# A transformer block with adapters on one core: the prologue's transfers, tables and first products in another order

## Chip, cores, metric

One core of a Trainium2 chip runs the whole program. The metric is the device time in microseconds; three executions of the kernel before took 955.52, 958.76 and 960.24 us, the median is 958.76. Engines: TensorE (PE) multiplies, VectorE (DVE), ScalarE (ACT) and GpSimd (POOL) work elementwise, SyncE (SP) issues DMA transfers.

## The reference

Eight sequences of 512 tokens with 256 features pass four layers. The first is a transformer layer whose normalisation is modulated by an embedding of a time step; then come an adapter chosen by a domain index, a rotation of groups of four features by two angles, and a second adapter. Cut to what matters here, with `_ln` a normalisation without weights:

```python
# layer 0; x is (8, 512, 256), 16 heads of 16
e = steps / 100 * 4000 * freqs                   # (8, 128)
emb = concat([sin(e), cos(e)])                   # (8, 256)
ada = silu(emb) @ W_ada + b_ada                  # (8, 512): scale, shift
h = _ln(x) * (1 + scale) + shift
q, k, v = h @ Wq + bq, h @ Wk + bk, h @ Wv + bv
s = q @ k.T / 4 + bias                           # bias is (8, 16, 512, 512)
s = where(mask, -inf, s)
x = h + softmax(s) @ v @ Wo + bo
# feed-forward with x * sigmoid(1.702 x); then the layers:
x = adapter1(x, domain); x = rotate(x, theta, phi); x = adapter3(x, domain)
```

## The kernel before

Work on attention is cut into 128 units: a sequence b, a group g of four heads and a tile qt of 128 queries. A unit loads four bias tiles of 128x512 (L856, 256 KB each), POOL adds the masked keys' large negative value (`neg`, L860), PE computes four scores matrices (L868), DVE subtracts them from the bias and takes row minima (L879), ACT takes the exponential (L883), the result is turned (by PE at L918, or by DVE at L894 and a transfer), and PE multiplies by the values (L944). After eight units half a sequence is complete, and `finish` runs the output projection, the feed-forward part and both adapters over it. While one sequence's units run, `prepare(b + 1)` makes q, k and v of the next.

Two parts set the order. The first lines (L286 to L328) are issued as they stand: SP's transfers of the first sequence, the small inputs and the first weights, memsets on POOL, `halves` on DVE. From `plan = Plan()` on, everything is a task of a planner: `plan(engine, cost, emit, reads, writes, mode, at)` notes a task with a cost in us, a `rank` (lower goes first), and where given an earliest time `at`. `plan.run` replays the engines as clocks that begin at the times in its argument and gives each free engine the ready task of lowest rank; DMA stands for SP's queue. `mode` adds a cost where an engine changes kind of work. `begin` and `end(first, last)` spread the ranks of the tasks between them. The result is one list, and each engine executes its instructions in that order: an instruction that waits holds all behind it on its engine. Weights are loaded into space that later holds other things: `first` is a view of a `pT` tile, with W_ada, Wq and Wk side by side.

The prologue's tasks by name. `embedding`: the token numbers are cast (`tokf`, L380), spread over partitions by a product with ones (L381), multiplied by frequencies and reduced to within pi (`reduced`, L387 to L395), then `sines` takes Sin twice, Square and Identity (L401 to L404), and a Tanh makes silu of it (L409, `emb` at L411). Filling products of the identity (`rows_of_identity`, L373) keep PE busy. `modulation`: `emb` by W_ada (L435), its sum with `b_ada` (L442), four transposes (L449) into columns `modc`. `constants`: bias columns `bk` and `bqh` (L469 to L477), and `dense`, which POOL uses to close the padding between heads in Wq and Wk (L492). `prepare(0)`: statistics of each token tile (L653, L655), the reciprocal root on POOL (L660 to L662), normalising on ACT (L675), transposes by PE (L739), modulation into `xT`, and into a turned copy `xTp` used for v (L753 on ACT, L755 on DVE), then for each of two chunks c of 128 padded columns q and k: products (L766), `qz` in two halves (L772) and `kT` (L782); then v (L803, L814) and `neg` from the mask (L819). Units of groups 0 and 1 read chunk 0, groups 2 and 3 chunk 1. `experts_matrices` gathers the adapters' expert weights (L1161 to L1197).

The compiler puts a table load (ACT_TABLE_LOAD) ahead of an activation whose function isn't in the table at hand.

Of the kernel before, what the change touches and what calls it, by code (L numbers as in the profile page):

```python
# [19 lines left out]
P = 128  # L20
# [195 lines left out]
def conditioned_sequence_kernel(  # L216
# [33 lines left out]
    def slots(name, count, shape, dtype=F32):  # L250
# [38 lines left out]
    nc.vector.memset(ang[:, B:], 0.0)  # L289
    nc.sync.dma_start(RES.tiles[0][:, :2], x0[:, :2])  # L290
    nc.sync.dma_start(cols, cols_in)
    nc.sync.dma_start(tok_i[:, :B], steps[None, :])
# [4 lines left out]
    nc.sync.dma_start(ang[:B, B:], angles.rearrange("(j b) -> b j", j=2))  # L297
    nc.sync.dma_start(tok_i[:, B:], domain[None, :])
    nc.sync.dma_start(
        SIG.tiles[0][:B].rearrange("p r d -> p (r d)"), rows_in[: 2 * D].partition_broadcast(B)  # L300
    )
    nc.sync.dma_start(first[:, 1], w_q.rearrange("(c p) n -> p c n", p=P))
    nc.sync.dma_start(first[:, 2], w_k.rearrange("(c p) n -> p c n", p=P))
# [16 lines left out]
    nc.gpsimd.memset(ones, 1.0)  # L320
    neg_half = const.tile([P, NT], F32, tag="neg_half", name="neg_half")
# [40 lines left out]
    def embedding():  # L362
# [6 lines left out]
        plan.rank = -4.9  # L369
# [5 lines left out]
        for _ in range(20):  # L375
            plan(PE, 0.28, rows_of_identity, [], [warm], mode="full")
# [3 lines left out]
        plan(DVE, 0.2, lambda: nc.vector.tensor_copy(tokf, tok_i), [], ["tokf"], at=4.2)  # L380
# [16 lines left out]
        plan(DVE, 1.2, reduced, [], [scr], at=5.0)  # L397

        def sines():
# [10 lines left out]
            th.t, sc[:, :, :B], AF.Tanh, scale=0.5), ["sc"], [th], mode="exp")  # L410
# [13 lines left out]
    def modulation():  # L424
# [5 lines left out]
            b_ada.t[:, 0], b_ada.t[:, 0], AF.Identity, bias=1.0), [], [b_ada], at=7.0)  # L430
# [8 lines left out]
        plan(PE, 2.2, product, ["emb"], [ps], mode="full", at=7.5)  # L439
# [20 lines left out]
    def constants():  # L460
# [5 lines left out]
            [], [further], mode="full", at=4.0)  # L466
# [15 lines left out]
        plan(DVE, 0.6, biases, [further], ["bk", "bqh"], at=4.2)  # L482

        for c in range(NC):
            for n, w in ((1, wq), (2, wk)):
# [8 lines left out]
                plan.rank = -9.0 + 0.1 * (n + 2 * c)  # L494
                plan(POOL, 0.55, dense, [], [("w", n, c)], at=7.5 + 1.2 * n)


        for i, v_pad in enumerate(VP.tiles):

            def clear(v_pad=v_pad):  # L500
                nc.gpsimd.memset(v_pad, 0.0)
                nc.gpsimd.memset(heads_of(v_pad)[:, :, :, HD : HD + 1], 1.0)

            plan.rank = -10.0
            plan(POOL, 2.0, clear, [], [("ones", i)])
# [11 lines left out]
    def late_weights():  # L517
# [6 lines left out]
        load(-2.5, 0.75, lambda: nc.sync.dma_start(  # L524
            wv, w_v.rearrange("(c p) n -> p c n", p=P)), "wv")
        load(-2.4, 0.4, lambda: nc.sync.dma_start(
# [803 lines left out]
```

## Time and profile before

| What | Measured |
|---|---|
| median of three executions | 958.76 us |
| the profiled execution, its time | 961.32 us |
| its span on the core | 959.6 us |
| mean granted PE clock | 0.987 |
| PE from 20 to 25 us | 4.54 of 5 us busy |
| PE from 25 to 30 us | 5.00 of 5 us busy |
| PE from 800 us to the end | 139.99 of 160 us busy |
| table loads on ACT | 1 each for L514, L401, L409; 27 for L1058, 26 for L883; 1283 ns each |
| first scores (L868) start | 24.91 us |
| scores of the ninth unit start | 67.0 us |

A row of the timeline has the start in us, the duration, the engine, the line and operation, what is written and read, the shape, how many instructions were joined, and in brackets the idle time of the engine before it with what ended it. A matrix product in float32 counts as two records. "PE busy" comes from modelled ends of products and overlaps with weight loads (PEld). The chain is followed back from the last instruction to what released each step, so a step on it is one that nothing else hid.

### The profile page before, as it was taken

What the parts mean: (1) busy time and instruction counts of PE and PEld (TensorE: products, weight loads), DVE (VectorE), ACT (ScalarE), POOL (GpSimd) and SP (SyncE); (2) the same over time, 40 slices, a digit from 0 to 9 for tenths busy, and PEclk for the clock granted to TensorE, in tenths of its full rate; (3) what the DMA queues carried; (4) which work ended last, traced back from release to release, by engine and by line L of the source; (5) the groups of instructions that cost most, each with busy time, mean ns of one, the idle gap of its engine ahead of it and who ended that gap; (6) DMA issues with size and microseconds to landing.
All of it is one profiled execution on the core that took longest, in us unless ns stands there. A gap on an engine that the chain in (4) does not pass through costs nothing.

```text
span 959.6 us, 21049 instructions
## 1 busy us (share of the span) xinstructions
PE 905.8 (94%) x6646; PEld 596.1 (62%) x6646; DVE 799.7 (83%) x2162; ACT 748.8 (78%) x1359; POOL 754.9 (79%) x841
## 2 busy tenths in 40 slices
PE   7999999999899999999999999999999999899993
PEld 4655765676565665666656665666656666566782
DVE  3786789987988889988898879987899888888755
ACT  5896879786887869879698778977788786897542
POOL 7788999787877969778887878878687886988222
PEclk9999999999999999999999999999999999999997
DMA  8579586987768787787969878688776978878000
GB/s 289 174 250 285 182 281 179 282 265 237 213 184 273 248 257 208 231 273 228 276 175 271 259 233 259 182 277 258 212 229 198 280 211 271 249 220 267 26 17 23
DMA packets 158945, 214.25 MB, mean 223 GB/s; under 512 B 18479, under 2 KB 90201, under 8 KB 158834
## 3 DMA queue, kind: packets, MB, share of 16 engines
q1 hardware_dynamic: 158834, 212.91, 73.2%
q8 instruction: 53, 0.87, 0.4%
q14 instruction: 58, 0.48, 0.1%
HBM read 149.89 MB, written 4.24 MB: 161 GB/s over the span
## 4 chain that ended last, share of the span: by engine, by line
PE 51%; DVE 16%; ACT 10%; POOL 7%; DMA 7%; issue 5%; SPq 1%; DVEq 0%; POOLq 0%; ACTq 0%
PE bank L1024 9%; PE bank L868 8%; PE bank L918 8%; PE bank L944 7%; PE bank L999 6%; DMA bias<-in_bias 6%; POOL bias L860 4%; DVE bias L879 4%; ACT bias L883 3%; PE bank L766 3%; DVE tb L894 3%; PE bank L711 2%; PE bank L803 2%; PE bank L1052 2%; PE bank L687 2%
## 5 line engine op out<-in xcount | busy, mean ns | idle before, releaser
L860 POOL TENSOR_TENSOR bias<-bias,neg 128x512 f32<-128x512 f32 x512 | 581.7, 1163 | 118.5 <-DMA bias<-in_bias 83.3
L883 ACT ACTIVATE bias<-bias,low 128x512 f32<-128x512 f32 x512 | 343.1, 720 | 67.7 <-DVE low L879 67.0
L879 DVE CUSTOM_DVE_ANT_0 bias<-bank,bias 128x512 f32<-128x512 f32 x512 | 326.7, 684 | 56.5 <-PE bank L868 49.4
L918 PE MATMUL bank<-shifted,bias 128*128 128x128 f32 x1152 | 160.9, 278 | 15.3 <-DVE inv L970 8.7
L918 PEld LDWEIGHTS bank<-shifted,bias 128*128 128x128 f32 x1152 | 128.9, 141 | 69.0 <-issue 16.9
L894 DVE STREAM_TRANSPOSE tb<-bias 128x512 f32<-128x512 f32 x224 | 150.1, 694 | 7.5 <-ACT bias L883 6.9
L868 PE MATMUL bank<-kT,qz 32*128 32x512 f32 x1024 | 156.0, 640 | 0.0
L645 ACT COPY pT<-bank 128x512 f32<-128x512 f32 x209 | 114.9, 586 | 30.8 <-PE bank L918 27.3
L944 PE MATMUL bank<-pT,v_pad 128*32 128x256 f32 x2048 | 125.0, 385 | 4.3 <-issue 1.4
L999 PE MATMUL bank<-hT,w 128*128 128x256 f32 (+1 forms) x544 | 123.5, 371 | 0.8 <-ACT pT L645 0.8
L1024 PE MATMUL bank<-w,gT 128*128 128x256 f32 x496 | 121.6, 382 | 0.0
L999 PEld LDWEIGHTS bank<-hT,w 128*128 128x128 f32 x544 | 95.4, 190 | 22.3 <-issue 8.4
L1024 PEld LDWEIGHTS bank<-w,gT 128*128 128x128 f32 x496 | 90.0, 190 | 26.1 <-issue 15.4
L944 PEld LDWEIGHTS bank<-pT,v_pad 128*32 128x32 f32 x2048 | 60.9, 110 | 66.7 <-issue 11.7
L868 PEld LDWEIGHTS bank<-kT,qz 32*128 32x128 f32 x1024 | 45.6, 183 | 48.4 <-issue 25.7
L1011 POOL TENSOR_SCALAR sig<-sig 128x512 f32<-128x512 f32 (+1 forms) x68 | 40.4, 597 | 39.7 <-ACT sig L1008 36.9
L1015 DVE SCALAR_TENSOR_TENSOR gT<-bank,cols,sig 128x256 f32<-128x256 f32 (+1 forms) x128 | 54.2, 464 | 14.8 <-POOL sig L1011 14.6
L1008 ACT ACTIVATE sig<-bank,b1s 128x256 f32<-128x256 f32 (+1 forms) x136 | 55.2, 454 | 10.1 <-PE bank L999 9.9
L653 DVE BATCH_NORM_STATS2 st<-res 128x6 f32<-128x256 f32 x128 | 52.3, 408 | 9.6 <-DMA res<-in_x 8.0
L675 ACT ACTIVATE bank<-res,rstd 128x256 f32<-128x256 f32 x64 | 36.3, 567 | 28.9 <-POOL rstd L662 24.8
L645 DVE COPY pT<-bank 128x512 f32<-128x512 f32 x79 | 52.1, 682 | 2.7 <-PE bank L918 2.6
L661 POOL TENSOR_TENSOR rstd<-rstd,neg_half 128x2 f32<-128x2 f32 (+2 forms) x59 | 43.5, 738 | 4.9
(145 smaller groups left out, 1117.7 us busy)
## 6 DMA issues: line engine op xcount, KB each, us to landing
bias<-in_bias SPq DMA_DIRECT2D x512, 256.0 KB, 3.9
pT<-tb SPq DMA_DIRECT2D x448, 128.0 KB, 3.0
out<-res SPq DMA_DIRECT2D x15, 256.0 KB, 2.9
res<-in_x SPq DMA_DIRECT2D x7, 512.0 KB
m<-in_mask SPq DMA_DIRECT2D x8, 256.0 KB, 3.8
mod<-ada_rows SPq DMA_DIRECT2D x8, 256.0 KB, 3.1
w<-in_w SPq DMA_DIRECT2D x2, 1024.0 KB
rot<-rot_rows SPq DMA_DIRECT2D x8, 256.0 KB
```

What stands on the lines that cost most here:

```text
L645: nc.scalar.copy(*pair()) if e == ACT else nc.vector.tensor_copy(*pair())), r, w)
L860: plan(POOL, 1.12, lambda j=j: nc.gpsimd.tensor_tensor(dif[j].t, dif[j].t, negs[qt].t, ALU.add), [negs[qt]], [dif[j]])
L868: nc.tensor.matmul(sc[j].t, qz.t[strip, par, c, qs], kT.t[strip, c, :], start=True, stop=True,)
L879: plan(DVE, 0.61, lambda j=j: nc.vector.tensor_tensor_reduce(dif[j].t, sc[j].t, dif[j].t, -1.0, 3.0e38, ALU.add, ALU.min, low.t[:, j : j + ...
L883: plan(ACT, 0.61, lambda j=j: nc.scalar.activation(dif[j].t, dif[j].t, AF.Exp, bias=low.t[:, j : j + 1], scale=-1.0), [(low, j)], [dif[j]] ...
L894: plan(DVE, 0.62, lambda j=j: nc.vector.transpose(tb.t.rearrange("p (m h k c) -> h p k m c", m=4, h=TURNED, k=NT)[j], dif[j].t.rearrange(" ...
L918: nc.tensor.transpose(ps.t[:, kc, :], dif[j].t[:, kc * P : (kc + 1) * P], ident)
L944: nc.tensor.matmul(pv.t[32 * j : 32 * j + 32, :], v_pad.t[:, at : at + 32], pj, start=(kc == 0), stop=(kc == NT - 1),)
L999: nc.tensor.matmul(ps.t[:, i, :w], w1[:, c, f * P : (f + 1) * P], hT.t[:, c, :w], start=(c == 0), stop=(c == NC - 1),)
L1008: plan(ACT, 0.155 + 0.1 * n, lambda i=i, f=f, ps=ps, sg=sg: nc.scalar.activation(sg.t[:, i, :w], ps.t[:, i, :w], AF.Tanh, bias=b1s[:, f : ...
L1015: plan(DVE, 0.14 + 0.13 * n, lambda i=i, f=f, ps=ps, sg=sg: nc.vector.scalar_tensor_tensor(gT.t[:, f, :w], ps.t[:, i, :w], cols[:, C_B1 + ...
L1024: nc.tensor.matmul(ps.t[:, i, :], gT.t[:, f, i * P : (i + 1) * P], w2[:, f, :], start=(f == 0), stop=(f == NF - 1),)
```

## The change

Only the prologue's order and a few ranks change; what is computed stays the same. Line numbers are those of the kernel before.

- The token numbers, the angles and `b_ada` are fetched by transfers that ACT issues, ahead of all its other work. SP keeps x, cols, W_ada, the mask, and of Wq and Wk the first half (the columns of chunk 0).
- The second halves of Wq and Wk become planned transfers with rank -1.9, behind the first unit's bias tiles (-2.0); `dense` of chunk 1 waits for them. Wv and its bias row get ranks -1.5 and -1.4 instead of -2.5 and -2.4.
- A one-element Silu activation comes first among ACT's functions, so that the table loaded for it is at hand when Sin and Tanh come; Tanh loses its `mode`.
- Of the filling products there are 42 instead of 20, at rank -2.45 instead of -4.9.
- The statistics of sequence 0 leave the stream and get rank -20.
- The first chunk of q is computed for the first 128 tokens alone, then k's chunk 0, then q for the other 384; the first unit's scores read only the first part.
- Earliest times, the ranks of `neg` and of the last expert steps, one POOL cost and the engines' starting times are changed.

```diff
+    nc.scalar.dma_start(tok_i[:, :B], steps[None, :])
+    nc.scalar.dma_start(tok_i[:, B:], domain[None, :])
+    nc.scalar.dma_start(ang[:B, B:], angles.rearrange("(j b) -> b j", j=2))
+    nc.scalar.dma_start(
+        SIG.tiles[0][:B].rearrange("p r d -> p (r d)"), rows_in[: 2 * D].partition_broadcast(B)
+    )
     nc.sync.dma_start(RES.tiles[0][:, :2], x0[:, :2])
     nc.sync.dma_start(cols, cols_in)
-    nc.sync.dma_start(tok_i[:, :B], steps[None, :])
     nc.sync.dma_start(RES.tiles[0][:, 2:], x0[:, 2:])
...
     nc.sync.dma_start(first[:, 0], w_ada.rearrange("(c p) n -> p c n", p=P))
-    nc.sync.dma_start(ang[:B, B:], angles.rearrange("(j b) -> b j", j=2))
-    nc.sync.dma_start(tok_i[:, B:], domain[None, :])
-    nc.sync.dma_start(
-        SIG.tiles[0][:B].rearrange("p r d -> p (r d)"), rows_in[: 2 * D].partition_broadcast(B)
-    )
-    nc.sync.dma_start(first[:, 1], w_q.rearrange("(c p) n -> p c n", p=P))
-    nc.sync.dma_start(first[:, 2], w_k.rearrange("(c p) n -> p c n", p=P))
+
+    def half_of(n, c):
+
+        src = (w_q, w_k)[n - 1].rearrange("(c p) n -> p c n", p=P)
+        cut = slice(c * 2 * P, (c + 1) * 2 * P)
+        nc.sync.dma_start(first[:, n, :, cut], src[:, :, cut])
+
+    half_of(1, 0)
+    half_of(2, 0)
...
+    silu = const.tile([1, 1], F32, tag="silu", name="silu")
+    nc.scalar.activation(silu, ones[:, :1], AF.Silu)
...
-        plan.rank = -4.9
+        plan.rank = -2.45
...
-        for _ in range(20):
-            plan(PE, 0.28, rows_of_identity, [], [warm], mode="full")
+        for i in range(42):
+            plan(PE, 0.22 if i > 6 else 0.48, rows_of_identity, [], [warm], mode="full")
...
-        plan(DVE, 0.2, lambda: nc.vector.tensor_copy(tokf, tok_i), [], ["tokf"], at=4.2)
+        plan(DVE, 0.2, lambda: nc.vector.tensor_copy(tokf, tok_i), [], ["tokf"], at=3.2)
...
-        plan(DVE, 1.2, reduced, [], [scr], at=5.0)
+        plan(DVE, 1.2, reduced, [], [scr], at=4.0)
...
-            th.t, sc[:, :, :B], AF.Tanh, scale=0.5), ["sc"], [th], mode="exp")
+            th.t, sc[:, :, :B], AF.Tanh, scale=0.5), ["sc"], [th])
...
-        plan(PE, 2.2, product, ["emb"], [ps], mode="full", at=7.5)
+        plan(PE, 2.2, product, ["emb"], [ps], mode="full", at=7.0)
...
-        plan(DVE, 0.6, biases, [further], ["bk", "bqh"], at=4.2)
+        plan(DVE, 0.6, biases, [further], ["bk", "bqh"], at=7.9)
+        plan.rank = -1.9
+        for n in (1, 2):
+            plan(DMA, 0.45, lambda n=n: half_of(n, 1), [], [("raw", n, 1)])
...
-                plan.rank = -9.0 + 0.1 * (n + 2 * c)
-                plan(POOL, 0.55, dense, [], [("w", n, c)], at=7.5 + 1.2 * n)
+                plan.rank = -9.0 + 0.1 * n + 6.0 * c
+                plan(POOL, 0.55, dense, [("raw", n, c)], [("w", n, c)], at=0 if c else 7.3 + 0.8 * n)
...
-        load(-2.5, 0.75, lambda: nc.sync.dma_start(
+        load(-1.5, 0.75, lambda: nc.sync.dma_start(
...
-        rstd = statistics(res, rk, range(NT), at=(4.0, 4.0, 4.8, 4.8) if b == 0 else None)
+        stream = plan.stream
+        if b == 0:
+            plan.stream, plan.rank = None, -20.0
+        rstd = statistics(res, rk, range(NT), at=(3.6, 3.6, 5.1, 5.1) if b == 0 else None)
+        plan.stream = stream
...
         for c in range(NC):
-            ps = chunk(wq, c, 1)
-            for u in range(2):
-                plan(ACT, 0.67, lambda ps=ps, c=c, u=u: q_out(ps, c, u), [ps, "bqh"], [(qz, u, c)])
-            ps = chunk(wk, c, 2)
...
+            early = b == 0 and c == 0
+            cuts = [slice(0, P), slice(P, S)] if early else [slice(0, S)]
+            for i, cut in enumerate(cuts):
+                ps = chunk(wq, c, 1, cut)
+                for u in range(2):
+                    plan(ACT, 0.24 + 0.43 * (cut.stop - cut.start) / S,
+                         lambda ps=ps, c=c, u=u, cut=cut: q_out(ps, c, u, cut), [ps, "bqh"],
+                         [(qz, u, c, "first") if early and i == 0 else (qz, u, c)])
+                if i == 0:
+                    ps = chunk(wk, c, 2)
...
-                at=9.5 if b == 0 else 0.0)
+                at=9.7 if b == 0 else 0.0)
         if b == 0:
             plan.end(-1.1, 1.5)
             for n, task in enumerate(plan.tasks[-NT:]):
-                task.rank = -7.0 + 1.5 * n
+                task.rank = (-5.0, -4.0, -0.5, 3.0)[n]
...
-        plan(PE, 0.98, scores, [(qz, par, c), (kT, c)], sc, mode="row")
+        plan(PE, 0.98, scores, [(qz, par, c) if n else (qz, par, c, "first"), (kT, c)], sc,
+             mode="row")
...
-            plan.rank = 5.0 + 4.0 * l
+            plan.rank = 9.0 + 2.0 * l
...
-    order = plan.run({PE: 2.0, DVE: 2.6, ACT: 2.2, POOL: 1.6, DMA: 7.0})
+    order = plan.run({PE: 1.5, DVE: 2.6, ACT: 3.6, POOL: 1.6, DMA: 5.0})
```

## The prediction

> **What bounds the kernel now.** I read the page's busy shares, then the busy time by stretches, then the chain that ended last, then the timeline of the first 30 us. On the page the engine with most work is TensorE:
>
> ```profile
> PE 905.8 (94%) x6646; PEld 596.1 (62%) x6646; DVE 799.7 (83%) x2162; ACT 748.8 (78%) x1359; POOL 754.9 (79%) x841
> ```
>
> Only the busy time by stretches tells where the other 6% lie (columns: stretch, its length, then PE, PE weight loads, DVE, ACT and POOL busy, the granted clock, the DMA share and GB/s):
>
> ```profile
> 5.00:10.00 5.00, 4.05 (x28) 3.57 (x28) 2.97 (x17) 1.58 (x2) 1.89 (x9) 1.00 1.03 335
> 10.00:15.00 5.00, 2.38 (x5) 0.37 (x4) 0.64 (x5) 4.90 (x14) 3.71 (x10) 0.80 0.92 321
> 15.00:20.00 5.00, 3.38 (x15) 1.48 (x14) 1.68 (x3) 3.12 (x6) 5.00 (x5) 0.86 1.02 384
> ...
> 100.00:200.00 100.00, 98.15 (x726) 63.96 (x730) 85.45 (x226) 80.93 (x144) 90.30 (x91) 1.00 0.77 234
> ```
>
> From 100 us on, PE is busy 98% of the time: a microsecond is won there only by taking work off PE, which this change doesn't. In the first 20 us it is busy two thirds of the time, part of that with filling products (L373), and from 10 to 20 us it runs at 0.80 and 0.86 of its clock. What sets the start of the attention stream is read from the chain (start, us, what):
>
> ```profile
> 3.47 3.12 DMA tok_i<-in_domain
> ...
> 8.85 1.27 ACT L401
> ...
> 10.88 1.28 ACT L409
> ...
> 12.63 3.24 PE bank L435 x4
> 15.87 0.02 issue
> 15.89 0.69 DVE sig L442
> ...
> 17.66 0.82 DVE xT L755
> 18.48 0.02 issue
> 18.51 1.27 ACT bias L753
> 19.78 0.54 ACT xT L753
> 20.32 0.14 issue
> 20.45 4.53 PE bank L766 x10
> 24.98 1.07 PE bank L868 x8
> ```
>
> A transfer of 32 bytes lands at 6.6; the embedding follows; two table loads sit inside it; its product runs cold; a turned copy of x (L753, 1.27) goes ahead of the second half of xT; three products with q and k weights stand ahead of the first scores (24.91).
>
> The other way into xT, in the timeline, is nearly as late: rstd ends at 13.5, but the four normalising activations wait behind the mask copies on ACT:
>
> ```profile
> 11.94 0.20 POOL L660 TENSOR_SCALAR rstd<-mv 128x4 f32<-128x4 f32 x1
> 12.39 2.17 ACT L819 ACTIVATE neg<-m 128x512 bf16<-128x512 uint8 x4
> 14.57 2.06 ACT L675 ACTIVATE res<-res,rstd 128x256 f32<-128x256 f32 x4
> 16.97 1.09 PE L739 MATMUL bank<-shifted,res 128*128 128x128 f32 x8
> ```
>
> **The measure.** PE is the bound later, so I count PE time without use up to the first scores. Busy to 24.9: 3.60+4.05+2.38+3.38+4.45 = 17.9. Filling products in the timeline took 3.36+1.20+2.72 = 7.3. L435's four records took 3.24, where four records of the same 128x512 form (L766) take 1.88 at full clock: 1.4 lost to the clock. Useful: 17.9-7.3-1.4 = 9.2, so 24.9-9.2 = 15.7 us were without use.
>
> **The change, part by part: the embedding's path.** Four small transfers go from SP to ACT's queue. Both token transfers are issued at about 0.7 and 1.1 instead of 1.73 and 3.47. With the same 3.12 to landing the later one lands at 4.2, with cols' 2.55 (issued 1.23, its reader starts at 3.78) at 3.6. ACT pays the issues: four of SP's 0.25 to 0.37, 1.3, hidden, as ACT did nothing but a table load until 3.78; the Silu activation's load then ends near 3.5. Cast to reduced angles took 2.07 (6.68 to 8.75), 0.4 of it biases, which move to 7.9: angles at 5.3 to 6.3. ACT needed 3.5 from there to tanh's end (8.84 to 12.37); with one table for Sin, Square and Tanh both 1.28 loads go, leaving 1.0: emb at 6.5 to 7.5 instead of 12.57.
>
> Next late is w_ada, whose landing nobody waited for. w_q landed 4.8 after its issue at 4.08, at 8.9; w_k, of equal size, about 1.9 later (its copy starts at 10.84). One such step back gives 7.0 for w_ada, a little less as it is issued 0.37 earlier. So the product starts at 7.0 to 7.5 and, with PE kept busy by more filling products, takes 1.88: end 9.2. From its end to modc before took 1.4 (15.87 to 17.26): modc at 10.6. If the cover by filling products failed, the 1.4 comes back here; the next path hides 1.3 of it.
>
> A rule that speaks against the first part: the Trainium skill ("DMA: Bandwidth & Descriptors", "Issuing engines are not separate DMA queues") says that issuing from several engines saves sequencer time alone, since the same DMA engines carry all of it. Here sequencer time is what delays: six SP issues stand ahead of the domain transfer, 2.7 us. By the rule nothing of the 3.12 shrinks, so my 4.2 stands and 3.6 falls; neither is on the path, as w_ada comes later.
>
> On the tables the Trainium skill ("ScalarE: Activation LUTs", "What ACT_TABLE_LOAD costs") prices a switch at 1283 ns plus a drain of about 1380. The rows show the load (1.28) and Sin starting at 10.13, right behind it, so no drain: two switches are worth 2.56 by the trace, 5.3 by the page.
>
> **The path of x becomes the longest.** Four statistics at a pitch of 0.52 take 2.1, the reduced angles about 1.7 between them; from 3.7 on DVE (first half of x was used at 3.61), the end is 7.5. The reciprocal root on POOL took 1.6 (11.94 to 13.53): 9.1, plus hops 9.3; POOL's clearing and corner work ended at 6.05 before, so it is free. ACT normalises in 2.06, now with no mask copy ahead: 11.4. Transposes 1.09: first half at 12.0, second at 12.5. xT 0.8 and 0.73: 12.8 and 13.3. Then k's first two products (0.94, from 12.8), q's last 128 columns (0.25), k's other two (0.94) end at 14.9 at most; kT costs 0.69: **first scores at 15.6** instead of 24.9. Modc at 10.6 has 1.4 us of slack against 12.0.
>
> What else must be there: half of w_k. Ahead of it and in it lie 1.5 MB instead of 2.1, so it lands where w_q did, 8.9, or, as rows of half the length have no row in the trace, at worst at w_k's 10.8; with POOL's 0.5 that is 11.3, before 12.8. The second halves go behind the first unit's bias loads: two more issues on SP (0.45 each), unused until the second q chunk. wv, bv and the next bias loads slide 1.9 behind them; bias tiles then landed every 0.65, and one unit's four take POOL 4.6, so the queue catches up. The first bias add waits for neg and its tile: neg follows normalising at 11.4+0.54, so POOL starts at 12 instead of 13.78. Moving the rank of the expert rows (5 to 9, 9 to 11) I cost at nothing: POOL's 1.2 there is covered until the adapter, which first comes after the eighth unit.
>
> **Added.** The 22 more products: until the scores 15.6-1.4 = 14.2 less 5.9 useful (9.2 without q's remaining three quarters, 1.4, and second chunk, 1.9) leave 8.3. Seven at the 0.48 that the first seven took (14 records in 3.36, two a product) and twenty at 0.247 (22 records in 2.72) fill that; 15 are left, with a rank ahead of q's remainder: 3.7 us behind the scores, of which some lies where PE would wait for the exponentials. The table for Exp, loaded at 10.88 before, now comes just ahead of the first exponential: 0 to 1.28. The later tables started without waiting for data, which speaks for the low end.
>
> **The sum**, from both sides. PE alone: without use were 15.7, now 15.6-5.9 = 9.7 and 3.7 of leftover products: 2.3 won. The stream of units: 24.9-15.6 = 9.3, less 1.28 for Exp's table: 8.0 won. The first is right where PE never starves later. But the stretches from 50 to 80 us show PE at 4.41, 4.52 and 2.96 of 5 while units wait; a stream that is ahead, with q, k and v products owed, puts those into such gaps. I take the middle, **5.2**. The profiled execution has 959.6 of span and 961.3 of time, 0.3% above the median of 958.76; the same subtraction gives 954.4 of span, and against the median 958.76-5.2 = **953.6**.
>
> **Rivals.** *PE's account holds entirely, or POOL does:* 2.3 won by the first count; by POOL's, whose 40 to 60 us are full, 13.78-12 = 1.8: 956.5 to 957. For it: PE is full from 25 to 50. Against: POOL idled 1.8 and 1.75 for bias tiles at 33 to 38, so it has room. *One table does not serve:* if Sin and Tanh need their own, emb comes 2.56 later, 1.3 of that covered by the slack: 3.9 won, 954.9. No row before shows a shared table. *Slower:* the order of all engines is one list, planned anew from shifted times, and SP is a queue in order. Behind a turned-tile transfer that waits for DVE (issued at 71.20) the bias loads came late and POOL stood:
>
> ```profile
> 76.86 3.40 POOL L860 TENSOR_TENSOR bias<-bias,neg 128x512 f32<-128x512 f32 x3 [3.14 <-DMA bias<-in_bias]
> ```
>
> PE lost 1.35 and 1.03 us there, 2.4 together. If the new order makes that once more in each of eight sequences, it costs 19 and ends at 958.8-5.2+19 = 972.6; from three such places on there is no gain, from five it is slower by over 0.5%. Against it: only this one place shows that size near the start, and the ranks of later work are untouched.
>
> **Chances.** 0.5% (4.8 us) is about what a measurement of this kernel can tell from no change. Forecast, a gain over 4.8: 0.52. PE's or POOL's account, or two tables, or a mild replanning loss, all within 4.8: 0.34. Slower by more: 0.14. The forecast's own range is 949 to 954; the unit stream whole and a gap or two closed give 948.5, one or two bad places after PE's account 961.5: that leaves out about 2 in 10.
>
> **What would show it.** After: tanh's end near 7, L435 near 7.2 in under 2 us at granted clock 1.0, one table load before 4 us and one before the first exponential, normalising before 11.5, first scores between 15 and 17. If L435 waits for its weights beyond 8, the transfers' order was the bound; if scores come before 17 and the ninth unit (67.0 before) less than 3 us earlier, the gain was given back to PE's owed work. I am wrong if the later stretches lose more PE time than before, or if DVE's reduced angles stand behind statistics that wait for x.

## The result, and the profile after

| | before | after |
|---|---|---|
| median, 20 runs each on the same chips | 960.11 us | 963.88 us |
| ratio, 95% interval | | 1.0028 [1.0007, 1.0049] |
| profiled execution: time, span | 961.32, 959.6 us | 965.51, 963.7 us |
| first scores start | 24.91 us | 18.40 us |
| ninth unit's scores start | 67.0 us | 69.7 us |

The changed kernel is slower by 0.28%, some 2.7 us; the forecast was 5.2 us faster. The prologue is quicker, as it was meant to be, and the time is longer all the same.

The page's first line, after:

```profile
PE 917.2 (95%) x6694; PEld 602.9 (63%) x6694; DVE 788.5 (82%) x2145; ACT 759.9 (79%) x1378; POOL 754.4 (78%) x841
```

PE has 11.4 us more of busy time than before (905.8), though the useful products are the same but for q's split; what was added is 22 filling products. The records of all filling products come to 13.5 us (7.3 before), so they make 6.2 of the 11.4; where the rest lies is not shown. Busy time by stretches, after (columns as before):

```profile
5.00:10.00 5.00, 5.00 (x28) 4.71 (x29) 2.65 (x18) 2.27 (x10) 3.28 (x12) 1.00 1.04 369
10.00:15.00 5.00, 5.00 (x34) 3.44 (x33) 2.11 (x4) 3.40 (x8) 2.09 (x5) 1.00 1.04 370
15.00:20.00 5.00, 5.00 (x32) 3.17 (x32) 0.60 (x2) 4.39 (x6) 5.00 (x6) 1.00 1.06 395
20.00:25.00 5.00, 5.00 (x27) 3.51 (x26) 4.21 (x16) 3.79 (x6) 5.00 (x6) 1.00 0.56 161
60.00:65.00 5.00, 3.27 (x8) 1.24 (x8) 1.61 (x6) 4.42 (x9) 2.65 (x3) 0.80 0.90 318
```

From 5 to 25 us PE is never idle, where it was busy 2.38 and 3.38 of 5. But what does it do? The chain that ended last, after (start, us, what); L384 is the filling products, L446 the product with W_ada, L893 the scores, L784 q and k:

```profile
1.29 2.31 DMA tok_i<-in_domain
...
5.20 4.61 PE bank L384 x26
9.81 1.81 PE bank L446 x4
11.62 1.09 PE bank L384 x8
...
14.08 1.12 PE bank L384 x10
...
17.36 1.11 PE bank L384 x10
18.47 1.07 PE bank L893 x8
19.54 2.43 PE bank L384 x20
21.97 3.87 PE bank L784 x10
25.84 1.07 PE bank L893 x8
```

Before, the chain ran through a transfer, table loads and turned copies; now it runs through PE from 4.1 us on, and the largest steps on it are filling products: 13 of them (two records each) ahead of L446, and ten between the first unit's scores and the work that the second unit needs. The covers became the path. ACT, in the timeline after, is as forecast:

```profile
2.24 1.28 ACT L331 ACT_TABLE_LOAD   x1 [2.24 <-DVE halves L338]
...
6.06 0.18 ACT L412 ACTIVATE sc<-bank 128x10 f32<-128x10 f32 x1 [1.34 <-DVE mv L669]
...
6.83 0.19 ACT L420 ACTIVATE bank<-sc 128x16 f32<-128x16 f32 x1
...
8.91 2.08 ACT L689 ACTIVATE res<-res,rstd 128x256 f32<-128x256 f32 x4 [1.57 <-POOL rstd L676]
10.89 2.17 ACT L844 ACTIVATE neg<-m 128x512 bf16<-128x512 uint8 x4
...
18.13 1.28 ACT L909 ACT_TABLE_LOAD   x1
```

One load serves Silu, Sin (L412) and Tanh (L420); normalising (L689) ends at 10.99. Later, at 60 us, a stall that the old order didn't have (the timeline after):

```profile
60.58 0.63 ACT L844 ACTIVATE neg<-m 128x512 bf16<-128x512 uint8 x1 [2.74 <-POOL bias L885]
...
61.11 2.52 ACT L659 COPY pT<-bank 128x512 f32<-128x512 f32 x5
...
61.73 0.66 PE L944 MATMUL bank<-shifted,bias 128*128 128x128 f32 x4 [2.05 <-ACT pT L659]
```

A mask copy for the next sequence waits 2.74 us for POOL to release its buffer, five copies of turned tiles stand behind it on ACT, and PE waits for those; then PE runs at half clock for 3.4 us (0.80 in the window above).

The page's first line shows another thing that the planner writes. Some tasks, mostly copies of turned tiles out of a bank, may run on either DVE or ACT, and the planner picks the engine as it goes: DVE has 17 instructions fewer than before (2145 against 2162) and 11.2 us less, ACT 11.1 us more (759.9 against 748.8). A new plan thus changes the order and this split together; where the text below speaks of a new order, the split comes with it.

How far is one execution ahead of another? A unit's start alone misleads, since an order may put other work ahead of it. So I added up PE's useful records (filling products left out, each weighted by its columns; the moments kept are those where weighting by rows and columns gives the same) and compared the moments at which the same share was done. Us behind (+) or ahead (-) of the kernel before:

```
at us      20    50    70   120   200   600   900
after    -3.8  -1.7  +1.6  +1.6  +3.3  +3.9  +2.8
```

The lead is 3.8 us at 20 us, 1.7 at 50, and gone at 70. These are single executions, and the time of one varies by some 4 us, so the table locates an early gain, not a loss of 2.7.

### The profile page after: what moved, and what is told of

It is laid out like the page before. It is cut to its first block, busy times and chain, and to the rows that moved or that the text cites. A ratio compares the mean times of both kernels' runs of the same rounds, so it can differ in the third digit from the quotient of the medians.

```text
span 963.7 us, 21131 instructions
## 1 busy us (share of the span) xinstructions
PE 917.2 (95%) x6694; PEld 602.9 (63%) x6694; DVE 788.5 (82%) x2145; ACT 759.9 (79%) x1378; POOL 754.4 (78%) x841
## 4 chain that ended last, share of the span: by engine, by line
PE 60%; ACT 14%; DVE 10%; DMA 6%; POOL 6%; issue 4%; SPq 1%; POOLq 0%; DVEq 0%; ACTq 0%
PE bank L1050 10%; PE bank L893 10%; PE bank L944 9%; PE bank L970 8%; PE bank L1025 7%; DMA bias<-in_bias 4%; ACT bias L909 4%; PE bank L784 3%; POOL bias L885 3%; PE bank L1078 2%; PE bank L701 2%; PE bank L725 2%; DVE bias L905 2%; ACT pT L659 2%; PE bank L828 2%
## 5 line engine op out<-in xcount | busy, mean ns | idle before, releaser
L905 DVE CUSTOM_DVE_ANT_0 bias<-bank,bias 128x512 f32<-128x512 f32 x512 | 328.4, 685 | 68.6 <-PE bank L893 58.5
L893 PE MATMUL bank<-kT,qz 32*128 32x512 f32 x1024 | 158.7, 642 | 0.0
L659 ACT COPY pT<-bank 128x512 f32<-128x512 f32 x220 | 120.5, 584 | 31.6 <-PE bank L944 30.4
L893 PEld LDWEIGHTS bank<-kT,qz 32*128 32x128 f32 x1024 | 47.1, 183 | 49.4 <-issue 27.8
L689 ACT ACTIVATE bank<-res,rstd 128x256 f32<-128x256 f32 x64 | 36.4, 568 | 22.6 <-POOL rstd L676 16.4
L659 DVE COPY pT<-bank 128x512 f32<-128x512 f32 x68 | 45.0, 680 | 3.2 <-PE bank L944 2.7
```

The lines of the kernel that those rows point to most:

```text
L659: nc.scalar.copy(*pair()) if e == ACT else nc.vector.tensor_copy(*pair())), r, w)
L893: nc.tensor.matmul(sc[j].t, qz.t[strip, par, c, qs], kT.t[strip, c, :], start=True, stop=True,)
L905: plan(DVE, 0.61, lambda j=j: nc.vector.tensor_tensor_reduce(dif[j].t, sc[j].t, dif[j].t, -1.0, 3.0e38, ALU.add, ALU.min, low.t[:, j : j + ...
```

## The experiments

Each ratio is to the kernel before on the same chip, with its 95% interval. The changed kernel was not run again beside them, so what is said against it is a quotient of two ratios, uncertain by some 0.3%. "Theory A" and "Rival B" are named anew in each expectation.

### The prologue's own steps

**Seven of the filling products ahead of L446 are not issued** (the changed kernel otherwise):

```diff
-        def rows_of_identity():
-            nc.tensor.matmul(warm.t, ident, ident, start=True, stop=True)
+        left_out = range(11, 18)
+        def rows_of_identity(i):
+            if i not in left_out:
+                nc.tensor.matmul(warm.t, ident, ident, start=True, stop=True)
```

> The changed kernel with its planned order kept, but seven of its filling products (the 12th to 18th, the last ones ahead of the embedding's product with W_ada) are not issued. Theory A (the filling products delay the path they are to keep warm: they run at 0.43 us each until 8.4, not at the planned 0.22, and the embedding's product waits in PE's order behind them although emb is ready at 7.56): the product starts at 7.6 to 7.9 instead of 9.74, at half clock, and ends 0.5 to 1.5 us earlier than 11.62; first scores (18.40) 0.5 to 1.5 earlier. Rival B (W_ada lands only near 9.7): the product starts at 9.6 to 9.8 as before and nothing moves. Either way the time changes by less than 0.2%, since PE's owed work is the same.

Measured 1.0007 [0.998, 1.0033]. PE in the timeline of this run:

```profile
4.86 2.91 PE L387 MATMUL bank<-shifted 128*128 128x128 f32 x12
7.70 3.18 PE L449 MATMUL bank<-pT,emb 128*8 128x512 f32 x4
```

The product starts at 7.70 with no wait, so W_ada was there. But it takes 3.18 instead of 1.88, since the clock was still at half (the trace's first full-clock record is at 10.4); it ends at 10.88, only 0.74 earlier, and the first scores come at 17.66, 0.74 earlier too.

**The kernel before, with the small transfers on ACT's queue and the one table alone:**

```diff
+    nc.scalar.dma_start(tok_i[:, :B], steps[None, :])
...
-    nc.sync.dma_start(tok_i[:, :B], steps[None, :])
...
+    nc.scalar.activation(silu, ones[:, :1], AF.Silu)
```

> The kernel before with its planned order kept; only the four small transfers go to ACT's queue and a Silu activation goes first, so that Sin and Tanh share a table. Theory A (the path of x through the mask copies on ACT, not the embedding's, was as late, and the body's order decides the rest): emb 4 to 5 us earlier than 12.4, the product starts between 7.5 and 9.7, but normalising still ends near 15.7, first scores 0 to 1.5 us earlier than 24.91; the time within 0.15% of the kernel before. Rival B (the embedding's path was the bound): first scores 3 us or more earlier, and 0.2% or more less time.

Measured 0.9984 [0.9959, 1.0009]: no change. PE in its timeline:

```profile
9.10 1.88 PE L437 MATMUL bank<-pT,emb 128*8 128x512 f32 x4 [0.39 <-DVE emb L413]
...
16.25 3.88 PE L768 MATMUL bank<-xT,wq 128*128 128x512 f32 x4 [0.54 <-DVE xT L757]
19.93 3.09 PE L768 MATMUL bank<-xT,wk 128*128 128x512 f32 x4
```

The product is 3.5 us earlier (12.63 before), normalising still waits behind the mask copies, and in between PE idles enough to lose its clock: q and k take 6.97, where four records of this form took 1.88 at full clock. First scores at 24.67: a path shortened beside a longer one.

**The kernel before, with the order of a few prologue tasks altered by hand** (normalising ahead of the masks, the root ahead of weight copies, the scores ahead of the second chunk) and the two edits of the last run; no more filling products:

```diff
     order = plan.run({PE: 2.0, DVE: 2.6, ACT: 2.2, POOL: 1.6, DMA: 7.0})
+    at = {t.n: t for t in order}
+    for n in [82]:
+        order.remove(at[n])
+        order.insert(order.index(at[81]) + 1, at[n])
...
```

> The kernel before, its planned order kept from the second unit on; small transfers on ACT's queue, one table, statistics' root and normalising put ahead of the mask copies and the weight copies, xT's second half ahead of the turned copy, the first scores ahead of q's and k's second chunk. No further filling products. Theory A (an early start without replanning and without paid filling products carries to the end): first scores at 18 to 20 instead of 24.91; PE time without use up to there falls from 15.7 to 11 to 13, so the last unit's scores 2.5 to 4.5 us earlier than 890.0 and the time 0.25 to 0.45% under the kernel before. Rival B (the first bias tiles land at 13.6 as before, and POOL, full later, holds the units): first scores at 18 to 20, but the ninth unit's (67.0) less than 1 us earlier, time within 0.15%.

Measured 1.0017 [0.9992, 1.0043]. First scores at 20.0 (4.9 earlier), the second unit's at 30.6 (29.6 before). PE's timeline shows why:

```profile
27.17 1.03 PE L920 MATMUL bank<-shifted,bias 128*128 128x128 f32 x4 [2.38 <-ACT bias L885]
```

Early scores meet a later stage that isn't ready: PE waits 2.38 us for the exponentials and then runs at half clock from 27.3 to 34.1. The ninth unit comes at 68.6 (67.0 before), and the gain of 0.25 to 0.45% that theory A forecast didn't come.

### Is an early or late start carried to the end?

**The ten filling products behind the first scores are not issued** (the edit of the first run, with `range(32, 42)`):

> The changed kernel, order kept, without the ten filling products that stand between the first and the second unit's scores. Theory A (PE is full from 15 to 45 us, so every filling product there is paid in full): the second unit's scores come 2.0 to 2.5 us earlier than 25.77, the third's and fourth's too, and the end is 1 to 2.5 us earlier (0.1 to 0.25%). Rival B (PE would have stood there for the exponentials anyway, and later units are set by other engines): second unit's scores less than 1 us earlier, end unchanged.

Measured 1.0016 [0.9987, 1.0045]. The second unit starts at 23.4 instead of 25.8, the fourth at 40.1 instead of 41.5, the last at 889.1 instead of 892.9 in the profiled execution; in the time nothing is resolved.

**Those ten issued four times each**, which by the records (9.20 below against 2.50) is 6.7 us more:

```diff
+            for _ in range(4 if i in range(32, 42) else 1):
```

> The changed kernel, order kept, with each of the ten filling products between the first and the second unit's scores issued four times: 30 more products, 7.4 us at 0.247 each. Theory A (from the first scores on PE's time is paid in full, so work that stands in front is carried to the end): the second unit's scores 7 to 7.5 us later than 25.77, the last unit's 6 to 8 later, the time 0.6 to 0.85% over that of the changed kernel (about 0.9 to 1.1% over the kernel before). Rival B (the body takes up a late start in its idle gaps, and an early one likewise): the last unit's scores less than 3 us later, the time less than 0.3% over the changed kernel's. Between the two, the share carried is read off.

Measured 1.0077 [1.0058, 1.0097], 0.49% or some 4.7 us over the changed kernel. PE in its timeline:

```profile
19.20 9.20 PE L385 MATMUL bank<-shifted 128*128 128x128 f32 x80
...
32.20 1.14 PE L894 MATMUL bank<-kT,qz 32*128 32x512 f32 x8
```

The second unit starts 6.4 us later than after, the eleventh 2.4, the fifteenth 1.1, and the last 1.4 earlier (891.5 against 892.9). So the profiled execution catches the delay up, while the median doesn't; that execution is the shortest of the six (962.7 us, median 968.75). The 0.49% has an interval of 0.2 to 0.8%: a part of a large delay is paid at the end, and how much is not settled.

**The mask copy of the stall at 60 us goes behind the five copies:**

```diff
+    at = {t.n: t for t in order}
+    for n in [215]:
+        order.remove(at[n])
+        order.insert(order.index(at[380]) + 1, at[n])
```

> The changed kernel with one ACT instruction moved: the second mask copy of sequence 1 (it waits 2.74 us for POOL at 57.8) is put behind the five copies of turned tiles that follow it on ACT. Theory A (the loss against the kernel before comes from stalls that the new order makes; this one holds up five copies that PE waits for, and the 2.05 us of PE idle time drops its clock to half for 3.5 us): the idle time at 59.7 falls below 0.7 us, the clock stays at 1.0, the eighth unit's scores come 3 to 4 us earlier than 65.1, the end 2 to 4 us earlier (0.2 to 0.4%). Rival B (later stalls take it up): eighth unit 3 to 4 us earlier, the last unit's scores (892.9) within 1 us.

Measured 1.0011 [0.9983, 1.004]. ACT's timeline there:

```profile
59.34 2.54 ACT L659 COPY pT<-bank 128x512 f32<-128x512 f32 x5 [0.49 <-PE bank L944]
61.73 0.67 ACT L844 ACTIVATE neg<-m 128x512 bf16<-128x512 uint8 x1
```

The stall is gone and the eighth unit starts at 62.7 instead of 65.1, though this execution began 1.0 later (first scores at 19.4). Its cause is shown; what it is worth at the end is within the noise.

**All 17 filling products left out and the mask copy moved:**

> The changed kernel, order kept, without the 17 filling products of the two earlier experiments and with the mask copy moved. Theory A (what the change lost stands in these three places): first scores near 17.7, second unit's near 22.6, eighth unit's at 58 to 60 instead of 65.1, last unit's 3 to 6 us earlier than 892.9, time 0.3 to 0.6% under the changed kernel's, at or under the kernel before. Rival B (given back later): last unit's scores within 2 us, time within 0.2% of the changed kernel's.

Measured 1.0059 [1.0036, 1.0082], no better than the changed kernel. The eighth unit starts at 61.3 (65.1 after), the last at 892.7 (892.9). In this execution the clock fell to half from 68.4 to 75.3 us, and the tenth unit is level again (74.2 against 74.0), so its trace can't tell what the lead of 3.8 us at 61 us is worth. The ratio, over ten executions, shows no gain: theory A, which put the loss in these three places, is refuted, and another thing costs the time.

### The order behind the prologue

**The kernel before with one line altered, the ranks of the expert steps:**

```diff
-            plan.rank = 5.0 + 4.0 * l
+            plan.rank = 9.0 + 2.0 * l
```

> The kernel before with one part of the change alone: the ranks of the last expert steps, 9 and 11 instead of 5 and 9. The prologue stays as it was, the planner makes another order from the eighth unit on. Theory A (a new order alone moves the end by as much as the whole change did, in either direction): the time differs from the kernel before by 0.2% or more, or the units' starts wander by 3 us or more against it between the tenth and the last, with PE gaps in other places. Rival B (the order of the body is of no account): every unit within 1.5 us of the kernel before, time within 0.15%.

Measured 1.0093 [1.0063, 1.0122], some 9 us. No task is added, but 14 instructions move from DVE (x2148, 2162 before) to ACT (x1373, 1359 before), 11.8 us of ACT's time. The two windows with the largest loss and the same two of the kernel before tell where PE waits (PE busy is the first number after the length). This run:

```profile
200.00:300.00 100.00, 92.14 (x662) 59.79 (x661) 80.19 (x218) 78.33 (x140) 80.72 (x90) 0.98 0.76 226
...
700.00:800.00 100.00, 94.85 (x702) 61.10 (x701) 84.14 (x230) 84.86 (x149) 80.30 (x88) 1.00 0.76 228
```

The kernel before:

```profile
200.00:300.00 100.00, 95.91 (x683) 61.95 (x684) 85.89 (x230) 80.30 (x146) 79.32 (x88) 0.98 0.76 227
...
700.00:800.00 100.00, 97.14 (x697) 64.06 (x694) 88.16 (x235) 83.65 (x150) 84.21 (x92) 1.00 0.77 230
```

3.8 and 2.3 us of PE are lost hundreds of microseconds behind a task at 9 to 11 in rank (over all eight windows from 100 to 900 us the loss is 5.8; two of them gain, 1.5 at most): the planner, meeting one task elsewhere, wrote another order for all that follows.

**Four more orders of the same work.** The filling products at rank 20 (only where nothing else wants PE); the kernel before with the changed start times; the changed kernel with the experts' ranks set back; and an order that the planner's own clock calls the worst of those tried (the last two pieces below; each of the others is one piece):

```diff
-        plan.rank = -2.45
+        plan.rank = 20.0
...
-    order = plan.run({PE: 2.0, DVE: 2.6, ACT: 2.2, POOL: 1.6, DMA: 7.0})
+    order = plan.run({PE: 1.5, DVE: 2.6, ACT: 3.6, POOL: 1.6, DMA: 5.0})
...
-            plan.rank = 9.0 + 2.0 * l
+            plan.rank = 5.0 + 4.0 * l
...
-        plan.rank = -2.45
+        plan.rank = -0.5
...
-    order = plan.run({PE: 1.5, DVE: 2.6, ACT: 3.6, POOL: 1.6, DMA: 5.0})
+    order = plan.run({PE: 1.8, DVE: 2.4, ACT: 3.6, POOL: 1.8, DMA: 5.0})
```

> The changed kernel, with the rank of the filling products raised from -2.45 to 20.0, so that the planner puts one of them only where no other task wants TensorE. The planner's own end (the last task on its own clock) is 906.07 us, against 907.75 for the kernel before and 911.56 for the changed one. Theory A (the order that the planner writes for the body decides the time, whatever the prologue does): the time follows the planner's end, some 1.7 us (0.2%) under the kernel before, so a ratio of 0.995 to 1.000, and 0.4 to 0.8% under the changed kernel's 1.0028. Rival B (the first scores' time decides): the first scores start no earlier than the changed kernel's 18.40, so the time is the changed kernel's, a ratio of 1.001 to 1.005.

> The kernel before, with only the times at which its planner takes each engine to be free at the start set to the changed kernel's (PE 2.0 to 1.5, ACT 2.2 to 3.6, DMA 7.0 to 5.0). No instruction is added, removed or altered; the planner writes another order. Its own end goes from 907.75 to 911.99. Theory A: slower than before by some 4 us, a ratio of 1.003 to 1.009. Rival B: nothing in the prologue is quicker or slower by over 1 us, so the same as before, 0.998 to 1.002.

> The changed kernel, with the experts' ranks set back to 5 and 9 (they are 9 and 11 in it). The planner's own end is 912.28 against 911.56. Theory A: no gain over the changed kernel, a ratio of 1.002 to 1.006 to the kernel before. Rival B (the expert ranks alone cost what was seen, since the kernel before with 9 and 11 took 1.0093): with them back, what the prologue wins is kept, so 0.993 to 0.999.

> The changed kernel with filling products of rank -0.5 and start times of the engines of PE 1.8, DVE 2.4, POOL 1.8: the worst order found by the planner's own clock, an end of 917.88, 6.3 us over the changed kernel's 911.56 and 10.1 over the kernel before's 907.75. The work is the changed kernel's. Theory A: 6 us (0.65%) over the changed kernel, a ratio of 1.007 to 1.013. Rival B: the prologue differs little, so the changed kernel's ratio, 1.001 to 1.005.

Measured: rank 20, 0.998 [0.9959, 1.0]; start times, 1.0034 [1.0014, 1.0054]; ranks back, 0.9988 [0.9966, 1.001]; worst, 1.0095 [1.0067, 1.0124]. Three went as theory A said. The start times alone are telling: no task is added, removed or altered, only their order and, for eleven of them, the engine (ACT x1370, 1359 before), and 0.34% is lost. The ranks set back went against A: the planner's clock had called that order worse, and it is better. It landed in the range of rival B, that the experts' ranks alone cost what was seen. Two other runs speak against that rival: rank 20 keeps the ranks 9 and 11 and is at 0.998, and the start times lose with the ranks 5 and 9. So the order matters, but the planner's clock doesn't rank orders that lie near each other.

### Prologue and order exchanged

The pair that parts the two. The changed prologue with the old order of every engine's work from 30 us on, and the old prologue with the changed kernel's. The planner is given a list for each engine and may start a listed task only when it heads its list:

```diff
+GIVEN = {"ACT": "263 264 182 183 184 ...", ...}
...
+                    if t.n in late and (not given[e] or given[e][0] != t.n):
+                        held.append(entry)
+                        continue
...
+                if t.n in late:
+                    given[e].pop(0)
```

> The changed kernel's prologue, with the order of every engine's work from 30 us on (5225 of 5422 tasks) taken from the kernel before, task by task. The planner's own end is 908.08 us (before 907.75, changed 911.56). Theory A (the order written for the body costs what the changed kernel lost): the loss goes, and of the prologue's 1 to 3 us something stays: a ratio of 0.996 to 1.000. Rival B (the prologue's own products and queues cost it): as the changed kernel, 1.001 to 1.005.

> The reverse: the kernel before's prologue, with the order of every engine's work from 30 us on taken from the changed kernel. The planner's own end is 912.75 us. Theory A: slower than the kernel before by what the changed kernel lost and its prologue hid, a ratio of 1.003 to 1.008. Rival B: nothing of the prologue is changed, so 0.998 to 1.002.

| ratio to before | old order from 30 us | new order from 30 us |
|---|---|---|
| old prologue | 1 | 1.0033 [1.001, 1.0057] |
| new prologue | 1.0008 [0.998, 1.0036] | 1.0028 [1.0007, 1.0049] |

Along a row the order costs 0.33 or 0.20%; down a column the prologue is worth +0.08 or -0.05%. Only the 0.33% is clear of noise: the difference of 0.20% is uncertain by 0.35, and the gain of up to 0.4% that theory A left for the prologue under the old order didn't show. The old prologue with the new order is as slow as the changed kernel, so the order suffices for the loss. Starts of units, us, show both sides:

```
unit              1st   3rd   4th   9th  15th   17th   19th   last
before           24.9  34.8  41.1  67.0 105.1  120.4  132.0  890.0
new prol, old o. 18.8  31.3  40.3  66.4 105.2  120.5  132.1  886.9
old prol, new o. 26.0  36.0  45.3  69.7 113.4  123.8  134.6  892.4
after            18.4  30.9  41.5  69.7 113.4  123.8  134.6  892.9
```

With the order given, two prologues whose first scores are 6 or 7.6 us apart reach the fifteenth unit within 0.1 us of each other, and the two kernels with the new order are 0.5 apart at the last. (The old prologue's 26.0 instead of 24.9 comes with the clock, at half from 12.4 to 15.8 and from 19.2 to 22.6 us in that execution, and only from 13.0 to 16.4 before. The 886.9 is one short execution, 960.08 us where its kernel's median is 962.22.) What takes the lead away, with the old order? Most of it, from 6.1 us at the first unit to 0.8 at the fourth, goes while PE is never idle. Busy time with the new prologue and the old order:

```profile
20.00:30.00 10.00, 10.00 (x58) 6.47 (x58) 7.07 (x24) 8.36 (x16) 9.76 (x11) 1.00 0.44 115
30.00:40.00 10.00, 10.00 (x83) 8.45 (x81) 5.93 (x15) 7.17 (x14) 5.27 (x6) 1.00 0.56 147
```

The scores were put ahead of products that PE still owed, and ten filling products, 2.5 us, stand behind them: by the count of useful records this kernel is 3.4 us ahead at 20 us and 0.7 at 50. The last 0.6 goes at two waits (PE's timeline):

```profile
75.81 1.93 PE L982 MATMUL bank<-pT,v_pad 128*32 128x256 f32 x32 [1.48 <-DMA pT<-tb]
...
80.21 0.44 PE L999 MATMUL bank<-shifted,pvs 128*128 128x128 f32 x2 [1.45 <-DVE pvs L671]
```

Before, the same two waits were 1.35 and 1.03: here they end on a transfer and on DVE, and whoever comes early waits longer.

**The two edits of order that helped, together** (rank 20 and the experts' ranks back), **and the exchanged kernel without the 17 filling products:**

> The changed kernel with both edits of rank that helped alone: filling products of rank 20 (0.9980 alone) and experts of ranks 5 and 9 (0.9988 alone). The planner's own end is 908.65 us, 2.6 above that of rank 20 alone. Theory A, with the planner's clock as the measure: slower than rank 20 alone, 0.999 to 1.003. If each edit takes its own share away, whatever that clock says: 0.993 to 0.997.

> As e13 (the changed prologue, the old order from 30 us on), and the seven filling products just ahead of the modulation's product and the ten after the first scores are not issued: second scores some 2.8 us earlier. If the prologue's gain carries to the end once the order is held: 1.5 to 3 us (0.15 to 0.3%) under e13, 0.994 to 0.998. If the body gives it back whatever the order: as e13 within 0.1%.

Measured 0.9993 [0.9969, 1.0018] and 1.0012 [0.9985, 1.0039]. The edits didn't add up, though the interval just reaches the 0.993 to 0.997 of a sum; each writes an order of its own. Without the 17 products the second unit is 1.4 us earlier (24.8 against 26.2), half of what was expected, as this run's first scores came 0.9 later; and PE idles longer afterwards (its timeline):

```profile
29.43 0.65 PE L959 MATMUL bank<-shifted,bias 128*128 128x128 f32 x4 [1.13 <-ACT pT L674]
```

By the ninth unit it is 1.2 behind, at 67.6. The body gives the lead back whatever its order.

The planner's own end and the split (DVE's instructions on the run's page) against the measured ratio, over all runs that write another order from ranks, start times or lists:

```
                        planner's end   on DVE   ratio
rank 20                     906.07       2158    0.9980
before                      907.75       2162    1
new prologue, old order     908.08       2163    1.0008
rank 20, ranks back         908.65       2163    0.9993
after                       911.56       2145    1.0028
start times alone           911.99       2151    1.0034
ranks back                  912.28       2143    0.9988
old prologue, new order     912.75       2144    1.0033
expert ranks alone          914.20       2148    1.0093
worst                       917.88       2139    1.0095
```

Every plan of the table that lost moved eleven or more instructions from DVE to ACT, and of the plans that did so only "ranks back" didn't lose. So the move alone doesn't make a loss. The two other plans that nearly keep the split, rank 20 without and with the ranks back, write new orders and don't lose either. Which of the two costs the time, the order or the split, is open.

The best is rank 20: 0.998 of the kernel before, an interval that just reaches 1, and by the two ratios 0.5% under the changed kernel.

## Why the prediction was wrong

**The expert ranks "cost at nothing": wrong, and decisive in kind.** The text looked for the cover of POOL's 1.2 us. It had to ask what the planner writes when the task moves: alone, the edit costs 0.93%. The same failed for the start times, which the text didn't cost at all: 0.34% alone. The rival "the order of all engines is one list, planned anew" had the mechanism. Its mild form, which came, shared a chance of 0.34 with three others, and its strong form had 0.14, because "the ranks of later work are untouched". That reason was false twice: the change does alter later ranks, those of the experts, and this planner's later choices, of order and of engine, hang on the times at which earlier work ends, whatever the ranks, as the start times alone show. The price, 2.4 us a place in eight places, was also of the wrong shape; the new order's measured loss is 0.33% behind the old prologue.

**The middle between PE's account and the stream of units: wrong.** The stream's 8.0 us is refuted: with the order held, first scores 6 us earlier changed the time by +0.8 us, with an interval from -1.9 to +3.5. The reason given for the upper half, that a stream ahead puts its owed products into later gaps, failed: PE had no gap from 20 to 40 us in which to catch up what it owed, and the gaps at 74 and 79 us end on a transfer and on DVE, and grew. The text's own test asked for a ninth unit at least 3 us earlier with first scores before 17. They never came before 17; the run with first scores at 17.66 had the ninth unit 1.1 earlier, the one with the order held 0.6.

**PE's account, 2.3 us: the better measure, mis-sized.** By the same count, after: first scores at 18.40 less 5.9 of useful work, and 2.43 of leftover products, makes 14.9 without use against 15.7, so 0.8 won instead of 2.3. With the order held the measured interval, from 1.9 us won to 3.5 lost, allows 0.8 and leaves out 2.3, if narrowly.

**First scores at 15.6: 18.40.** The product was forecast to end at 9.2 and ended at 11.62. "PE kept busy by more filling products" was taken as cover only. They stand ahead of the product in the list, at half clock they take twice as long (the first ten records 2.50 us, behind the scores twenty in 2.50), and without them the product itself runs at half clock. The x transposes then follow the product and eight more records, so they came at 12.55 and not at 11.4. PE was the prologue's path, and the forecast had followed that of x over DVE, POOL and ACT.

**Right:** one table (tanh's end 7.02, forecast near 7); no table load ahead of Sin; normalising ended at 10.99 (11.4); W_ada there by 7.70 (7.0 landing); Exp's load hidden at 18.13 (0, of 0 to 1.28). The leftover products took 2.43, within the 3.7 allowed. The late token transfer landed at 3.60, 2.31 after its issue, where the text kept 3.12 and 4.2. That POOL starts at 12 was too early: 13.93, after the second halves' weight copies.

**Open:** whether the order itself or the split between DVE and ACT costs the time, and at which places in the body. The stall at 60 us is one, and taking it out didn't change the time measurably. Both kernels with the new order are 2.6 us behind at the 19th unit, but one execution varies by more than the loss. Part of that scatter goes with the granted clock: of the twelve executions without the ten products behind the first scores, the shortest, 959.58 us, had 0.991 and the longest, 970.76, 0.983.

## What to carry to other kernels

Where a scheduler writes the order, every edit of a rank, a cost or a start time is an edit of the whole program: compare the written orders and which engine got each task, and hold both for the rest before crediting a stage. Filling products are work on the engine that they warm; putting them behind everything else that engine could do gave the best ratio here, though how much of it the new order gave is not shown. A lead at the start counts only if the engine that bounds the time owes less work at that moment, and only up to the next wait that ends on another engine or a transfer.

## What the hardware showed

The full clock came at different times in kernels whose first 7 us on PE are alike. The trace's first full-clock record is at 8.4 us after the change, at 11.0 with the mask copy moved and at 10.6 with rank 20, with PE busy from 1.4 us on but for 0.2 us. The Trainium skill ("TensorE: Matmul & The Clock Gate", "What's actually happening") expects full clock after about 3.4 us of sustained work, in a window that runs freely. An estimate from that page, two windows behind 1.4, gives 8.2 at the latest; these runs are later, and the measurement decides.

The clock also fell after idle times shorter than that page's window: after 2.05 us at 60 us, for 3.41 us, and after 2.38 at 25 us, for 6.83. Not every such wait is followed by a fall: after 3.04 us at 10 us with the changed start times, and after 2.55 at 163 us with rank 20 and the ranks back, the clock stayed. Where it falls, a half-clock stretch of 3.41 or 6.83 us costs, as an estimate, up to another 1.7 or 3.4 us of PE's work.
